# A gated feed-forward kernel on Trainium2: weights of three slots loaded into buffers of their own, sums kept as rows and dealt to GpSimd, two more slots by seven products

## The chip, the cores and the metric

The kernel runs on one core of a Trainium2 chip. A core has five engines that work side by side, each on a queue of its own in order: TensorE (PE, matmuls; PEld is its loading of weights), VectorE (DVE), ScalarE (ACT), GpSimd (POOL) and SyncE (SP, which here issues nearly all DMA transfers). They meet through semaphores. SBUF is the memory that all of them work on, PSUM the eight banks that PE writes its sums to. The metric is the device time of one execution in microseconds (us), median of the runs.

## The reference

The core of it, with x of shape (4, 1024, 512), cond (4, 128), norm_w (512, 128), up_w (4096, 512) and down_w (512, 2048), all f32:

```python
scale = cond @ norm_w.T + 1.0
ms = jnp.mean(x * x, axis=-1, keepdims=True)
h = x * (scale[:, None, :] * jax.lax.rsqrt(ms + EPS))
u = h @ up_w.T
val, gate = jnp.split(u, 2, axis=-1)
h = val * jax.nn.gelu(gate, approximate=False)
hq = act_quant(h)        # 8 bits, one scale per token
wq = weight_quant(down_w)   # -1, 0, 1 times one scale
return hq @ wq.T + x
```

The first product (`h @ up_w.T`) is f32 and is the large part. The second has small integers on both sides.

## The kernel before

**Batches, slots, halves.** The four batches of 1024 tokens are taken one after the other. In each, the 2048 gate and 2048 value features are cut into NJ = 16 slots of 128 gate and 128 value features. A batch's tokens are two halves of TOK = 512. Every f32 operand is kept as a high and a low f16 part and a product is three f16 terms (high by low, low by high, high by high).

**Two ways to compute a slot.** `plain_half` makes one half of a slot directly: twelve matmuls of 512 columns for the gate (`plain`, L1137) into bank A or B, a Gelu on ACT (L1161), twelve for the value into bank E, and a DVE step (L1165) that multiplies both and so empties bank E. A slot is 48 matmuls. `slot` makes both halves at once by seven products of six matmuls (`product`, L1122), 42 a slot, in the manner of Strassen's scheme: it needs sums and differences of the quarters of the weights and of the input, and ACT and DVE copy and add banks between the products (L1200, L1208, L1212; L1220, L1230, L1236, L1239). Of PSUM's banks A and E have two each, B one, and three ("po") serve transposes and small things. In the first batch the slots below SEVEN = 14 are plain and the last two use `slot`; the later batches use `slot` throughout. The plain halves come in the order (0,0), (1,0), (2,0), (0,1), (1,1), (2,1), (3,0), (3,1), (4,0) and so on, (slot, half).

**Weights, once, during the first batch.** For slot j: `w_load` (L747) brings 512 KB of up_w; `w_largest` (L757 on ACT, or L759 on DVE for the first slots) and `w_factor` (L766 to L769) find a power of two for each row; `w_scale` (L788 on ACT, L790 on POOL) multiplies by it; `w_rows` (L813 on ACT, L814 on DVE) splits the result in high and low part and transposes it by DMA into the slot's f16 tile. Slots 0 to 2 are transposed on PE instead (`w_turn`, `w_high`, `w_low`), and `w_evac` (L839) copies the transposed f32 values out of PSUM. `s_sums` (L847 to L850) makes the four sums that the seven products need, from the scaled weights as loaded (slots 3 on) or from what `w_evac` kept (slots 0 to 2); `s_high` (L861, ACT) and `s_low` (L865, DVE or POOL) split them; `s_spill` writes the slot's tile to DRAM, where batches 1 to 3 read it by `s_load_x` and `s_load_y`. The sums of slots 3 to 13 lie in DRAM as rows and are transposed by the DMA that loads them; those of slots 0 to 2, 14 and 15 lie transposed. The natural weights of all slots share three buffers in turn, `W_SLOT`: H[12], H[13] and H[14]. H (18 slots of 128 x 1024 f32) is also the store of the results of the slots.

**Input.** The first batch's x lies in H[4] to H[7]. Its first half is prepared at the start; of the other half `first_sum` takes the sums of squares, `rsqrt` (L982, L983) the root, `first_scale` (L1468 on ACT, L1470 on POOL) scales, `first_turn` (L1475) transposes on PE, `first_high` (L1479, ACT) and `first_low` (L1483, DVE) write the two parts.

**What sets the order.** The program isn't emitted as written. Each call is first recorded by a planner (`Plan`), which knows what depends on what, has a price for each operation (`price`) and a lag for each hand-over between engines (`lag`), works out when each result is needed, and places all steps, PE's foremost. It then tries a list of small alterations, one for each seed in `MENDS`, each of which moves steps ahead of which PE waited in its own replay. The outcome is a fixed order for each engine. Each engine works its list strictly in order: a step that waits holds up everything behind it.

Of the kernel before, what the change touches and what calls it, by code (L numbers as in the profile page):

```python
# [22 lines left out]
P = 128  # L23
# [92 lines left out]
class Plan:  # L116
# [284 lines left out]
    100002, 100010, 100012, 100045, 100056, 100059, 100066, 100072, 100095, 100096, 100105, 100124,  # L401
    100140, 100188, 100274, 100292, 100370, 100398, 100424, 100470, 100489, 100678, 100785, 101115,
    101696, 102543,
# [38 lines left out]
def lag(s, t):  # L442

    if s.eng == t.eng:
        return 0.0
    if s.eng == "PE":
        return 0.2
    return 0.08 if t.eng == "POOL" else 0.05


def price(eng, method, writes, reads, args, kwargs):
# [25 lines left out]
    if method == "reciprocal":  # L477
        return 0.15 + max(0, wide - 8) * 0.0055, False, 0.0
    if wide <= 32:
        return 0.14, not psum, 0.0  # L480
# [40 lines left out]
def glu_quant_kernel(  # L521
# [142 lines left out]
    def cond_scale_rest():  # L664

        n = B - 1
        v = H[:, 9:11].rearrange("p s h t -> p (s h t)")[:, : n * NK * C]
# [42 lines left out]
    def cond_rows():  # L710

        n = NK * B
        pr, v = po_bank("pr", [n, P]), H[:n, 8, 0, 64 : 64 + P]
# [18 lines left out]
    W_SLOT = {1: 12, 2: 13, 0: 14}  # L732
# [3 lines left out]
    def wn(j):  # L736
        return H[:, W_SLOT[j % 3]]

    def wf(j):

        return H[:, 11 if j == 2 else 15 + j % 2].rearrange("p t (n f) -> p (t n) f", n=2)
# [39 lines left out]
    SEVEN = 14  # L781

    def w_scale(j, ts=(1, 0), eng=None):
        eng = eng or (ACT if j >= ROWS else POOL)
# [17 lines left out]
    def a_parts(j):  # L802

        s = s_tile(j)
        return s[:, 5:7], s[:, 3] if j >= ROWS else A21[:, j % 3], s[:, 4]
# [31 lines left out]
    def w_evac(j):  # L837
        for n in range(2):
            ACT.copy(wf(j)[:, 2 * n : 2 * n + 2].rearrange("p n f -> p (n f)"), pw[j][n])  # L839

    def s_sums(j):
        if j >= ROWS:
            v = wn(j).rearrange("p t (n f) -> p t n f", n=2)
            a11, a12, a21, a22 = v[:, 1, 0], v[:, 1, 1], v[:, 0, 0], v[:, 0, 1]
        else:
            a11, a12, a21, a22 = (wf(j)[:, n] for n in range(4))
        DVE.tensor_tensor(sf[:, 0], a21, a22, ALU.add)  # L847
        DVE.tensor_tensor(sf[:, 2], a11, a21, ALU.subtract)
        DVE.tensor_tensor(sf[:, 1], sf[:, 0], a11, ALU.subtract)
        DVE.tensor_tensor(sf[:, 3], a12, sf[:, 1], ALU.subtract)  # L850

    def s_parts(j):
# [3 lines left out]
        s4 = A21[:, j % 3 : j % 3 + 1] if j >= ROWS else s[:, 3:4]  # L856
# [718 lines left out]
    def first_batch(j, sc):  # L1575
# [34 lines left out]
        for f in FIRST_T.get(j, ()):  # L1610
            f()
# [473 lines left out]
```

## Time and profile before

| | us |
|---|---|
| median of 3 runs | 731.36 (731.32 to 731.37) |
| the profiled execution | 731.21 |
| its span | 729.2 |
| busy: PE, DVE, ACT, POOL | 719.0, 616.4, 410.0, 120.5 |

The span is what the profiler's records cover; the execution's own time is 2.0 us longer. The profile's rows are groups of instructions: line, engine, operation, output <- input, shape, count, then busy time in us, the mean of one in ns, and the idle time ahead of them with what ended it. In rows of the timeline the first number is the start, the second the duration, and a bracket gives the wait ahead. The ends of matmuls are modelled, so durations of PE rows overlap the next row; their starts are good. The last batch ends with the second product's tail; the change leaves its code alone.

### The profile page before, as it was taken

What the parts mean: (1) busy time and instruction counts of PE and PEld (TensorE: products, weight loads), DVE (VectorE), ACT (ScalarE), POOL (GpSimd) and SP (SyncE); (2) the same over time, 40 slices, a digit from 0 to 9 for tenths busy, and PEclk for the clock granted to TensorE, in tenths of its full rate; (3) what the DMA queues carried; (4) which work ended last, traced back from release to release, by engine and by line L of the source; (5) the groups of instructions that cost most, each with busy time, mean ns of one, the idle gap of its engine ahead of it and who ended that gap; (6) DMA issues with size and microseconds to landing.
All of it is one profiled execution on the core that took longest, in us unless ns stands there. A gap on an engine that the chain in (4) does not pass through costs nothing.

```text
span 729.2 us, 10150 instructions
## 1 busy us (share of the span) xinstructions
PE 719.0 (99%) x3655; PEld 358.4 (49%) x3655; DVE 616.4 (85%) x916; ACT 410.0 (56%) x671; POOL 120.5 (17%) x116
## 2 busy tenths in 40 slices
PE   8999999999999999999999999999999999999998
PEld 4544444444444446655444445665444444445744
DVE  7988898989898789968789888688879889956898
ACT  5776875773656785554433777733333676332454
POOL 2411222210000004570001300660001000000010
PEclk9999999999999999999999999999999999999999
DMA  7379687999767796777543446669543334443414
GB/s 253 119 236 216 159 227 232 233 251 262 237 208 169 190 184 184 192 161 177 136 129 92 95 101 188 159 156 181 120 101 102 102 101 102 102 101 101 149 44 155
DMA packets 185805, 116.77 MB, mean 160 GB/s; under 512 B 147718, under 2 KB 155287, under 8 KB 185756
## 3 DMA queue, kind: packets, MB, share of 16 engines
q1 hardware_dynamic: 185466, 115.81, 62.3%
q8 instruction: 28, 0.46, 0.3%
q10 hardware_dynamic: 290, 0.33, 0.1%
q14 instruction: 21, 0.17, 0.1%
HBM read 58.15 MB, written 23.09 MB: 111 GB/s over the span
## 4 chain that ended last, share of the span: by engine, by line
PE 83%; DVE 10%; ACT 3%; issue 2%; POOL 1%; DMA 1%; SPq 0%; DVEq 0%; ACTq 0%; POOLq 0%
PE A L1122 33%; PE E L1122 17%; PE po L1394 9%; PE B L1122 8%; PE E L1137 6%; PE B L1137 3%; PE A L1137 3%; DVE H L1315 2%; DVE am L1283 1%; DMA wd<-xr 1%; DVE H L814 1%; ACT H L788 1%; ACT H L813 1%; DVE R L1352 1%; ACT xr L950 1%
## 5 line engine op out<-in xcount | busy, mean ns | idle before, releaser
L1122 PEld LDWEIGHTS <-SXY 128*128 128x128 f16 x2016 | 197.2, 98 | 233.2 <-issue 1.9
L1122 PE MATMUL A<-R,SXY 128*128 128x512 f16 x1140 | 264.0, 379 | 1.0 <-ACT t L1200 0.9
L1122 PE MATMUL E<-R,SXY 128*128 128x512 f16 x570 | 138.7, 379 | 0.0
L1315 DVE TENSOR_TENSOR H<-H,am 128x1024 f32<-128x1024 f32 x64 | 77.6, 1235 | 0.1
L1122 PE MATMUL B<-R,SXY 128*128 128x512 f16 x288 | 70.3, 379 | 0.0
L1256 DVE TENSOR_REDUCE gm<-H 128x512 f32<-128x1024 f32 x56 | 68.9, 1231 | 0.9
L1137 PEld LDWEIGHTS <-SXY 128*128 128x128 f16 x438 | 42.8, 98 | 53.2 <-issue 2.3
L1272 POOL PARTITION_ALL_REDUCE am<-R x8 | 16.6, 2078 | 287.8 <-DVE R L1258 254.9
L1220 DVE SCALAR_TENSOR_TENSOR H<-A,sg,t 128x512 f32<-128x512 f32 x50 | 37.4, 749 | 28.5 <-PE A L1122 27.9
L1200 ACT COPY t<-A 128x512 f32<-128x512 f32 x50 | 29.2, 584 | 56.0 <-PE A L1122 56.0
L1233 ACT ACTIVATE t<-t,sg 128x512 f32<-128x512 f32 x50 | 36.1, 721 | 43.0 <-DVE t L1230 42.5
L1208 ACT COPY B<-A 128x512 f32<-128x512 f32 x50 | 28.5, 571 | 50.7 <-PE A L1122 50.3
L1394 PE MATMUL po<-wd,R 128*128 128x256 fp8e4 (+1 forms) x448 | 56.8, 275 | 0.0
L1217 ACT ACTIVATE t<-B,sg 128x512 f32<-128x512 f32 x50 | 34.3, 687 | 39.0 <-PE B L1122 38.7
L1230 DVE TENSOR_TENSOR t<-E,t 128x512 f32<-128x512 f32 x50 | 34.5, 689 | 24.6 <-PE E L1122 24.1
L1394 PEld LDWEIGHTS <-R 128*128 128x128 bf16 (+1 forms) x480 | 47.0, 98 | 12.8
L1236 DVE TENSOR_TENSOR v<-A,v 128x512 f32<-128x512 f32 x50 | 34.5, 689 | 20.0 <-PE A L1122 17.7
L1137 PE MATMUL E<-R,SXY 128*128 128x512 f16 x210 | 48.9, 379 | 1.1 <-DVE H L1165 1.1
L1212 ACT COPY v<-E 128x512 f32<-128x512 f32 x50 | 29.2, 585 | 29.5 <-PE E L1122 18.4
L1323 ACT ACTIVATE H<-H 128x1024 f32<-128x1024 f32 x38 | 39.8, 1050 | 9.7 <-DVE H L1315 9.6
L1239 DVE SCALAR_TENSOR_TENSOR H<-v,sg,t 128x512 f32<-128x512 f32 x50 | 39.8, 797 | 2.4 <-ACT t L1233 2.1
L1327 ACT ACTIVATE R<-H 128x1024 bf16<-128x1024 f32 x38 | 39.5, 1053 | 0.5
(268 smaller groups left out, 959.8 us busy)
## 6 DMA issues: line engine op xcount, KB each, us to landing
SXY<-s_dram SPq DMA_DIRECT2D x55, 256.0 KB, 2.7
H<-in_L_cond_up_w_dram SPq DMA_DIRECT2D x13, 512.0 KB, 4.0
s_dram<-SXY SPq DMA_DIRECT2D x16, 384.0 KB, 3.1
SXY<-s_dram SPq DMA_DIRECT2D x13, 384.0 KB, 3.2
xr<-in_x_dram SPq DMA_DIRECT2D x19, 256.0 KB, 3.2
out_dram<-xr SPq DMA_DIRECT2D x19, 256.0 KB, 2.2
H<-in_x_dram SPq DMA_DIRECT2D x8, 512.0 KB
SXY<-s_dram SPq DMA_DIRECT2D x29, 128.0 KB, 2.2
```

The lines of the kernel that those rows point to most:

```text
L1122: PE.matmul(o, s[:, w, k, :], xs(l, k), start=start and n == 0, stop=stop and n == len(TERMS) - 1, skip_group_check=True,)
L1137: PE.matmul(ps, a[k // 2][:, w, k % 2, :], XP[:, l, k, h * TOK : (h + 1) * TOK], start=n == 0, stop=n == len(terms) - 1,)
L1220: DVE.scalar_tensor_tensor(h_half(g - 1, 0), prev["A"], gain(g - 1, 0), prev["t1"], ALU.mult, ALU.mult)
L1230: DVE.tensor_tensor(prev["t2"], prev["E"], prev["t2"], ALU.add)
L1233: ACT.activation(prev["t2"], prev["t2"], AF.Gelu, scale=gain(g - 1, 1))
L1236: DVE.tensor_tensor(cur["v"], cur["A"], cur["v"], ALU.add)
L1239: DVE.scalar_tensor_tensor(h_half(g - 1, 1), prev["v"], gain(g - 1, 0), prev["t2"], ALU.mult, ALU.mult)
L1256: DVE.tensor_reduce(gm[0], v, AX.X, ALU.max, apply_absolute_value=True)
L1315: DVE.tensor_tensor(v, v, r.to_broadcast([P, 2, TOK]), ALU.mult)
L1323: ACT.activation(v, v, AF.Copy, bias=MAGIC)
L1327: ACT.activation(q, by_tile(v), AF.Copy, bias=-MAGIC)
L1394: PE.matmul(po, w[:, j], m, start=start and j == 0, stop=stop and j == n - 1, skip_group_check=True,)
```

## The change

There are five edits. The order tables that follow show the two engines whose lists move most.

- `W_SLOT` becomes a list: the natural weights of slots 3, 4 and 5 get H[8], H[9] and H[10], so that their loads need not wait for a buffer of slots 0 to 2. Scratch of the condition (`cond_scale_rest`, `cond_rows`), which lay there, moves into R[:, 1].
- `w_evac` goes, and with it the special case of slots 0 to 2: their sums are made from the scaled weights as loaded and kept as rows in DRAM like those of slots 3 on. So `s_load` transposes for slots 0 to 11 instead of 3 to 13, and the spill of slots 0 to 2 is in three pieces instead of one.
- Work is dealt out anew: `s_sums` runs wholly on POOL for slots 0 to 3 and half on POOL for 4 and 5 (all was on DVE); `w_scale` runs on POOL up to slot 4 (was up to 2).
- SEVEN is 12 instead of 14: slots 12 and 13 of the first batch are made by `slot`, and their sums are transposed ahead of the spill. For slots above 12 `w_rows` stands ahead of `s_all`.
- The planner's numbers in `lag` and `price` and its list of seeds change.

```diff
@@ MENDS @@
-26 seeds from 100002 to 102543
+40 seeds from 23000004 to 23011637
@@ lag @@
+    if s.eng == "PE":
+        return 0.0 if t.eng == "PE" else 0.2
     if s.eng == t.eng:
-        return 0.0
-    if s.eng == "PE":
-        return 0.2
-    return 0.08 if t.eng == "POOL" else 0.05
+        return {"DVE": 0.1, "ACT": 0.08, "POOL": 0.07}.get(s.eng, 0.0) if not s.wait else 0.0
+    return 0.05 if s.wait else 0.13 if t.eng == "POOL" else 0.1
@@ price @@
-        return 0.15 + max(0, wide - 8) * 0.0055, False, 0.0
+        return 0.08 + max(0, wide - 8) * 0.006, False, 0.0
     if wide <= 32:
-        return 0.14, not psum, 0.0
+        return 0.08, not psum, 0.0
@@ cond_scale_rest, cond_rows @@
-        v = H[:, 9:11].rearrange("p s h t -> p (s h t)")[:, : n * NK * C]
+        v = R[:, 1, 4096 : 4096 + n * NK * C]
...
-        pr, v = po_bank("pr", [n, P]), H[:n, 8, 0, 64 : 64 + P]
+        pr, v = po_bank("pr", [n, P]), R[:n, 1, 1536 : 1536 + P]
@@ weights @@
-    W_SLOT = {1: 12, 2: 13, 0: 14}
+
+    W_SLOT = [14, 12, 13, 8, 9, 10, 14, 12, 13] + 3 * [14, 12, 13]
     def wn(j):
-        return H[:, W_SLOT[j % 3]]
-
-    def wf(j):
-
-        return H[:, 11 if j == 2 else 15 + j % 2].rearrange("p t (n f) -> p (t n) f", n=2)
+        return H[:, W_SLOT[j]]
...
-    SEVEN = 14
+    SEVEN = 12
...
-        eng = eng or (ACT if j >= ROWS else POOL)
+        eng = eng or (ACT if j >= 5 else POOL)
...
-        return s[:, 5:7], s[:, 3] if j >= ROWS else A21[:, j % 3], s[:, 4]
+        return s[:, 5:7], s[:, 3], s[:, 4]
...
-    def w_evac(j):
-        for n in range(2):
-            ACT.copy(wf(j)[:, 2 * n : 2 * n + 2].rearrange("p n f -> p (n f)"), pw[j][n])
-
     def s_sums(j):
-        if j >= ROWS:
-            v = wn(j).rearrange("p t (n f) -> p t n f", n=2)
-            a11, a12, a21, a22 = v[:, 1, 0], v[:, 1, 1], v[:, 0, 0], v[:, 0, 1]
-        else:
-            a11, a12, a21, a22 = (wf(j)[:, n] for n in range(4))
-        DVE.tensor_tensor(sf[:, 0], a21, a22, ALU.add)
-        DVE.tensor_tensor(sf[:, 2], a11, a21, ALU.subtract)
-        DVE.tensor_tensor(sf[:, 1], sf[:, 0], a11, ALU.subtract)
-        DVE.tensor_tensor(sf[:, 3], a12, sf[:, 1], ALU.subtract)
+        v = wn(j).rearrange("p t (n f) -> p t n f", n=2)
+        a11, a12, a21, a22 = v[:, 1, 0], v[:, 1, 1], v[:, 0, 0], v[:, 0, 1]
+        (POOL if j < 4 else DVE).tensor_tensor(sf[:, 0], a21, a22, ALU.add)
+        (POOL if j < 4 else DVE).tensor_tensor(sf[:, 2], a11, a21, ALU.subtract)
+        (POOL if j < 6 else DVE).tensor_tensor(sf[:, 1], sf[:, 0], a11, ALU.subtract)
+        (POOL if j < 6 else DVE).tensor_tensor(sf[:, 3], a12, sf[:, 1], ALU.subtract)
...
-        s4 = A21[:, j % 3 : j % 3 + 1] if j >= ROWS else s[:, 3:4]
-        return (s[:, 0:3], sf[:, 0:3]), (s4, sf[:, 3:4])
+        return (s[:, 0:3], sf[:, 0:3]), (A21[:, j % 3 : j % 3 + 1], sf[:, 3:4])
@@ s_spill, s_load_x, s_load_y @@
-        if j < ROWS or j >= SEVEN:
+        if j >= SEVEN:
...
-        s_load(g, 0, Y_FROM, ROWS <= w_of(g) < SEVEN)
+        s_load(g, 0, Y_FROM, w_of(g) < SEVEN)
...
-        if not ROWS <= w_of(g) < SEVEN:
+        if w_of(g) >= SEVEN:
@@ first_batch @@
+        if SEVEN < j and n < NJ:
+            w_rows(n)
         if n < NJ:
             s_all(n)
         if j + 3 < NJ:
             w_scale(j + 3)
-            w_rows(j + 3)
+            if j < SEVEN:
+                w_rows(j + 3)
@@ third_slot, after plain_first @@
-        w_evac(2)
...
-    w_evac(0)
-    w_evac(1)
```

In the tables a row is line, operation, output <- input and shape, with a count where a row repeats; lines of the changed kernel are about nine lower than before. First POOL around the root for the other half of the input (`rs_0_88`). Before:

```order
L790 TENSOR_SCALAR H<-H,iv_96 128x512 x2
L790 TENSOR_SCALAR H<-H,iv_103 128x512
L790 TENSOR_SCALAR H<-H,iv_104 128x512 x2
L983 TENSOR_TENSOR rs_0_88<-ssq_0_87,neghalf 128x4
L1470 TENSOR_SCALAR H<-H,rs_0_88 128x512 x2
L982 TENSOR_SCALAR ssq_114<-ssq_114 128x2
L983 TENSOR_TENSOR rs_115<-ssq_114,neghalf 128x2
```

The same place after the change (L839 to L842 are the sums, L856 the low parts, L1461 `first_scale`):

```order
L789 TENSOR_SCALAR H<-H,iv_103 128x512
L842 TENSOR_TENSOR H<-H 128x256
L856 TENSOR_TENSOR SXY<-H,SXY 128x3x256
L839 TENSOR_TENSOR H<-H 128x256
L840 TENSOR_TENSOR H<-H 128x256
L789 TENSOR_SCALAR H<-H,iv_104 128x512 x2
L974 TENSOR_TENSOR rs_0_88<-ssq_0_87,neghalf 128x4
L856 TENSOR_TENSOR R<-H,R 128x256
L1461 TENSOR_SCALAR H<-H,rs_0_88 128x512
L841 TENSOR_TENSOR H<-H 128x256
L1461 TENSOR_SCALAR H<-H,rs_0_88 128x512
L842 TENSOR_TENSOR H<-H 128x256
```

The two input scalings stood directly behind the root; now a low part and a sum stand between.

Second, ACT from the Gelu of half (1,1) to that of half (2,1). Before:

```order
L1161 ACTIVATE t_0_105<-A_89,sg_78 128x512
L861 CAST R<-H 128x256
L861 CAST R<-H 128x3x256
L813 CAST H<-H 128x4x256
L1161 ACTIVATE t_1_106<-A_91,sg_78 128x512
```

After, from the second step behind the Gelu of (1,1) on (the first is another cast of a high part, `L852 CAST SXY<-H 128x3x256`); L756 is `w_largest`, L787 `w_scale`, L812 `w_rows`, L852 `s_high`:

```order
L852 CAST R<-H 128x256
L756 ACTIVATE R,wam_102<-H 128x512 x2
L756 ACTIVATE R,wam_95<-H 128x512
L812 CAST H<-H 128x4x256 x2
L756 ACTIVATE R,wam_95<-H 128x512
L756 ACTIVATE R,wam_102<-H 128x512
L787 ACTIVATE H<-H,iv_96 128x512
L852 CAST SXY<-H 128x3x256
L787 ACTIVATE H<-H,iv_103 128x512 x2
L787 ACTIVATE H<-H,iv_96 128x512
L756 ACTIVATE R,wam_102<-H 128x512
L1152 ACTIVATE t_1_106<-A_91,sg_78 128x512
```

Three steps stood between the two Gelus; now there are fifteen.

Third, ACT at the entry to slot 12. Before, when slot 12 is plain:

```order
L1161 ACTIVATE t_1_106<-A_89,sg_78 128x512
L788 ACTIVATE H<-H,iv_104 128x512 x2
L813 CAST H<-H 128x3x256
L861 CAST SXY<-H 128x3x256
L1161 ACTIVATE t_0_105<-B_90,sg_78 128x512
L861 CAST R<-H 128x4x256
L757 ACTIVATE R,wam_95<-H 128x512 x2
```

After (L1199 copies bank A to B, L1203 bank E to SBUF, L1191 bank A to SBUF, L1208 is `slot`'s Gelu):

```order
L1152 ACTIVATE t_1_106<-A_89,sg_78 128x512
L852 CAST R<-H 128x4x256
L1199 COPY B_90<-A_91 128x512
L756 ACTIVATE R,wam_95<-H 128x512 x2
L1203 COPY v_120<-E_101 128x512
L1191 COPY t_0_121<-A_91 128x512
L787 ACTIVATE H<-H,iv_96 128x512
L1208 ACTIVATE t_0_105<-B_90,sg_78 128x512
L787 ACTIVATE H<-H,iv_96 128x512
L1199 COPY B_90<-A_89 128x512
```

A cast of 1024 values and the copy to bank B are now neighbours, and three copies out of PSUM stand among the weight steps.

More of the change, by code (lines that the diff above doesn't have):

```diff
@@ L400 @@
 MENDS = (
-    100002, 100010, 100012, 100045, 100056, 100059, 100066, 100072, 100095, 100096, 100105, 100124,
-    100140, 100188, 100274, 100292, 100370, 100398, 100424, 100470, 100489, 100678, 100785, 101115,
-    101696, 102543,
[5 rows of a table added]
 )
```

5 rows, old and new, of the table MENDS are left out of this document.

## The prediction

> **What bounds the kernel now.** I read the page's head first, then busy time by stage, then what TensorE waited for.
>
> ```profile
> span 729.2 us, 10150 instructions
> PE 719.0 (99%) x3655; PEld 358.4 (49%) x3655; DVE 616.4 (85%) x916; ACT 410.0 (56%) x671; POOL 120.5 (17%) x116
> ...
> core 0: us, PE busy (x) PEld busy (x) DVE busy (x) ACT busy (x) POOL busy (x), PEclk, DMA share, GB/s
> 24.00:90.00 66.00, 63.70 (x303) 29.59 (x302) 59.52 (x126) 50.04 (x91) 16.02 (x15) 1.00 0.67 176
> 90.00:146.50 56.50, 56.50 (x263) 25.64 (x262) 51.29 (x89) 38.31 (x69) 14.72 (x10) 1.00 0.93 227
> 146.50:167.20 20.70, 20.70 (x98) 9.41 (x96) 17.57 (x37) 15.75 (x28) 3.40 (x4) 1.00 0.95 251
> ```
>
> TensorE (PE) is busy 99% of the span, so there are two ways to gain: fewer matmuls, or less of the little time in which PE waits. The stage rows say where that time is: 2.3 us of the 66 us from 24 to 90 (first batch, about slots 0 to 6), nothing from 90 to 167.2, where the slots that follow end. There DVE is busy 59.5 of 66 us, ACT 50.0, POOL 16.0: DVE is the next bound, POOL has room. The granted clock is 1.00 in all. What PE waited for, over the whole run (us in total, times, longest):
>
> ```profile
> PE E L1137 <- DVE H L1165: 1.5, 3, 1.1
> PE A L1122 <- ACT t L1200: 0.9, 2, 0.7
> PE B L1137 <- ACT t L1161: 0.6, 1, 0.6
> PE B L701 <- DVE dg L695: 0.4, 1, 0.4
> PE po L685 <- DVE mx L678: 0.2, 1, 0.2
> ```
>
> L1137 is `plain`, L1165 the vector operation that empties bank E of a plain half, L1161 its Gelu. Both of the large waits stand in PE's timeline between 66 and 87 us:
>
> ```profile
> 66.59 2.75 PE L1137 MATMUL A<-R,SXY 128*128 128x512 f16 x12
> 70.43 2.75 PE L1137 MATMUL E<-R,SXY 128*128 128x512 f16 x12 [1.08 <-DVE H L1165]
> ...
> 80.82 2.75 PE L1137 MATMUL E<-R 128*128 128x512 f16 x12
> 84.19 2.75 PE L1137 MATMUL B<-R,SXY 128*128 128x512 f16 x12 [0.62 <-ACT t L1161]
> ```
>
> A group of twelve shows 2.75 us because its last matmul's end is modelled; the cost of a matmul is read from the chain of waits, where nothing is late:
>
> ```profile
> 164.64 2.59 PE E L1137 x12
> 167.23 1.29 PE A L1122 x6
> ```
>
> 2.59/12 = 1.29/6 = 0.216 us a matmul. By starts, 70.43 - 66.59 = 3.84 and 84.19 - 80.82 = 3.37, against 2.59: the two slips are 1.25 and 0.78. Each exceeds its printed wait by 0.16, the modelled end. With L1165's two short waits (0.4) and the two of the condition (0.6) as printed, five gaps, 24 to 90 loses 2.3 + 5 x 0.16 = 3.1 us.
>
> **The change part by part.** Slots 12 and 13 by seven products: 42 matmuls instead of 48 each, so 12 x 0.216 = **-2.6**, sure as long as PE stays the bound there. Beside it each slot adds three ACT copies from PSUM and two DVE additions, and takes none off the path. Prices of these and of what follows, from the groups by form (busy, mean ns, idle ahead):
>
> ```profile
> L847 DVE TENSOR_TENSOR H<-H 128x256 f32<-128x256 f32 x16 | 8.8, 549 | 3.9 <-POOL SXY L865 2.1 <-POOL R L865 1.1 <-issue 0.6
> L848 DVE TENSOR_TENSOR H<-H 128x256 f32<-128x256 f32 x16 | 6.7, 417 | 0.0
> L1165 DVE SCALAR_TENSOR_TENSOR H<-E,sg,t 128x512 f32<-128x512 f32 x27 | 19.8, 741 | 2.3 <-POOL H L1105 2.2
> L1236 DVE TENSOR_TENSOR v<-A,v 128x512 f32<-128x512 f32 x9 | 6.2, 688 | 2.0 <-PE A L1122 2.0
> ...
> L788 ACT ACTIVATE H<-H,iv 128x512 f32<-128x512 f32 x27 | 18.4, 715 | 10.8 <-DVE iv L769 10.6
> L757 ACT ACTIVATE R<-H 128x512 bf16<-128x512 f32 x20 | 12.5, 626 | 0.9 <-DMA H<-in_L_cond_up_w_dram 0.6
> L813 ACT CAST H<-H 128x1024 f16<-128x1024 f32 x11 | 11.5, 1043 | 0.3
> L861 ACT CAST SXY<-H 128x768 f16<-128x768 f32 x10 | 8.3, 827 | 3.4 <-DVE H L849 2.8 <-issue 0.6
> L1208 ACT COPY B<-A 128x512 f32<-128x512 f32 x10 | 5.7, 570 | 5.7 <-PE A L1122 5.3
> L861 ACT CAST R<-H 128x256 f16<-128x256 f32 x12 | 4.9, 404 | 10.5 <-DVE H L850 10.5
> L757 ACT ACTIVATION_READ_ACCUMULATOR R<-H 128x1 f32 x20 | 3.8, 188 | 0.0
> L861 ACT CAST R<-H 128x1024 f16<-128x1024 f32 x2 | 2.1, 1036 | 2.1 <-issue 2.1
> ```
>
> Three copies of 0.57 and two additions of 0.69 fit in the idle time that 146.5 to 167.2 has today (ACT 5.0, DVE 3.1 for two slots: 3.4 and 2.8), only just. At the entry to slot 12 the copy B<-A, for which the next product but one waits, is queued on ACT behind a 1024-wide high part: 1.04 + 0.57 = 1.6 us against the 1.29 of the product that covers it. **+0.3** (0 if the high part runs early, 1.2 if both copies meet such a step).
>
> Sums: twenty of the 24 of slots 0 to 5 go from DVE to POOL. At L848's 0.42 (L847's 0.55 holds waits on POOL) DVE is rid of 20 x 0.42 = 8.4 us; the six evacuations of w_evac (L839, priced like L1208: 3.4) and the four scalings of slots 3 and 4 (2.9) leave ACT. The two engines that the slips of 24 to 90 waited on thus get 8.4 and 6.3 us back where they had 6.5 and 16 idle, against slips of 1.25 at most. I take all five as gone: **-3.1** (ends: 0 and -3.1).
>
> What is late next is what waits for POOL, which gets 20 sums, four scalings and the other half's two input scalings in one row:
>
> ```profile
> L790 POOL TENSOR_SCALAR H<-H,iv 128x512 f32<-128x512 f32 x5 | 3.4, 691 | 8.9 <-DVE iv L769 8.8
> ...
> 26.38 2.94 POOL L1470 TENSOR_SCALAR H<-H,rs 128x512 f32<-128x512 f32 x2
> 302.19 0.72 POOL L1037 TENSOR_TENSOR H<-H 128x256 f32<-128x256 f32 x1
> ...
> 31.09 1.84 ACT L1479 ACTIVATE R<-po,scT 128x512 f16<-128x512 f32 x3 [0.35 <-PE po L1475]
> ...
> 33.91 2.75 PE L1137 MATMUL A<-R,SXY 128*128 128x512 f16 x12
> ```
>
> L1037's 302.19 has the shape of a sum: 0.72 us on POOL. First place: behind POOL's rsqrt, a low part of 256 (about a sum's size, with its lock waits 0.8) and a sum now stand ahead of the second input scaling: 0.8 + 0.7 = 1.5 us later. The high parts L1479 that hang on it end at 31.09 + 1.84 = 32.93 today and are first read at 33.91: 1.0 free. **+0.5** (0 if the two steps run before the rsqrt is ready, 1.0 if ACT's own queue adds to it).
>
> Second place: ACT between the Gelus of halves (1,1) and (2,1), where the order shows one cast of 256 then six w_largest (6 x 0.81), two w_rows (2.1), four scalings (2.9), two casts of 768 and the one of 256 (2.1 together): 12.0 us. With both Gelus (0.68 each) and L1165 (0.74) that is 14.1 from the end of gate (1,1). PE has six groups, 15.5 us, until value (3,1) needs the bank of (2,1); with 0.2 of handing over, 1.2 us are free. The casts wait for POOL's sums of slot 3, and the queue with them: nothing if these are done before, four sums and two scalings (4.3) if all come in a row. The middle is 2.1, and 2.1 - 1.2 = **+0.9** (0 to 3.1).
>
> Other slots, 2 to 11: today's order left slips of 0.1 to 1.2, another order on engines with more idle time leaves some. **+0.3** (0 to 1.2).
>
> Hidden: three early weight loads (512 KB each) in free buffers ahead of slot 3; kept rows, which turn three more slots' loads in batches 1 to 3; six further spill pieces. Their cover:
>
> ```profile
> SXY<-s_dram SPq DMA_TRANSPOSE x58, 3.9
> ```
>
> A turned load lands 3.9 us after issue, within a slot of 42 x 0.216 = 9.07 us; that leaves 5 us before it shows, and if the buffer came free so late, all nine loads would cost their excess. From 90 to 167 the queues are 0.93 to 0.95 busy while PE loses nothing; there the change takes the spills of 12 and 13 from full to two halves. The waits on L1200 (0.9) lie after 263 us, where the order hardly moves. Startup: early loads compete with the input tiles; 0 (-0.3 to +0.5).
>
> Sum on the profiled execution (731.21; span 729.2, the rest lies around it): -2.6 - 3.1 + 0.5 + 0.9 + 0.3 + 0.3 = -3.7, so 727.5. The median of the runs is 0.15 above that execution: **727.6**.
>
> **The rivals.** *All is hidden.* POOL's row is served in time everywhere: 731.4 - 2.6 - 3.1 = 725.7. For it: POOL idle for 50 of 66 us today. Against: its steps are nearly twice DVE's (0.72 to 0.42).
>
> *The gain turns into waits on POOL.* The second place costs its upper end, 3.1, and the first 1.0: 731.4 - 5.7 + 4.1 + 0.6 = 730.4, range 728.8 to 731.5. For it: one ACT queue, twelve steps deep, hangs on POOL. Against: the sums can be made as soon as the weights are scaled, and these come early now.
>
> *DVE and POOL block one another, and it gets slower.*
>
> ```profile
> 90.57 3.00 POOL L1105 TENSOR_TENSOR H<-H 128x1024 f32<-128x1024 f32 x1 [1.67 <-DVE H L1105]
> ...
> 91.39 2.46 DVE L847 TENSOR_TENSOR H<-H 128x256 f32<-128x256 f32 x1
> 94.11 0.41 DVE L849 TENSOR_TENSOR H<-H 128x256 f32<-128x256 f32 x1
> ...
> 318.35 1.18 POOL L1036 TENSOR_TENSOR xt<-xn 128x256 f32<-128x256 f32 x1
> ...
> 318.86 1.21 DVE L1239 SCALAR_TENSOR_TENSOR H<-v,sg,t 128x512 f32<-128x512 f32 x1
> ```
>
> A sum on DVE took 2.46 us while a POOL operation on two SBUF inputs ran (to 93.57), and 0.41 beside none. So the moved sums, 20 x 0.72 = 14.4 us on POOL, hold DVE up for a share f of that time: net -8.4 + 14.4f. At f = 0.58 nothing is gained; at f = 1 the stretch loses 6.0, 731.4 - 2.6 + 6.0 = 734.8, the old slips kept. Slower by over 1.5 us needs f above 0.87. Against: only DVE steps with two SBUF inputs show it, and L1165, the Gelu and PSUM work do not belong to them; at 318, where both engines ran such steps back to back, POOL's 1.18 exceeds 0.72 by 0.46, so they shared the loss. I put f at 0.3.
>
> [...]
>
> **How the numbers follow.** All hidden 0.22 (725.7); the forecast's case 0.50 (726.6 to 728.9, likeliest 727.6); waits on POOL 0.18 (half of it under 729.9); blocking 0.10. Fewer than 2 in 10 lie outside 725.3 to 731.2. 0.2% is 1.5 us, about what can be told from no change, with the bounds at 729.9 and 732.8: faster 0.22 + 0.50 + 0.08 = 0.80, same 0.12 (the rest of the third, 0.02 of the blocking), slower 0.08.
>
> **What would show it.** Right: 12 fewer matmuls; PE's waits on L1165 and L1161 between 24 and 90 gone or under 0.5 together; DVE's busy time there down by some 4 us (8.4 - 14.4 x 0.3), POOL's up by about 15; waits of ACT's casts on POOL sums before about 60. Wrong: PE waits of over 2 us near 57 behind a late cast, sums or low parts on DVE of 1 us and more, PE waits on turned loads after 170, or a start later by more than 0.5.

## The result, and the profile after

The changed kernel takes 723.56 us (median of 4 runs, 723.48 to 723.75), the kernel before 731.37: the ratio is 0.9894 with a 95% interval of 0.9876 to 0.9911, so 7.8 us are gained where 3.8 were forecast, and the time lies below the range that was given. The profiled execution took 723.53 with a span of 721.7. The head of its page, with busy time, share and count of each engine:

```profile
span 721.7 us, 10147 instructions
...
PE 715.4 (99%) x3643; PEld 357.3 (50%) x3643; DVE 609.9 (85%) x899; ACT 407.4 (56%) x665; POOL 135.1 (19%) x139
```

Its stages (start:end, length, then busy time and instructions of PE, PEld, DVE, ACT, POOL, granted clock, DMA share, GB/s):

```profile
0.00:24.00 24.00, 21.10 (x102) 10.80 (x103) 19.36 (x71) 12.63 (x27) 11.74 (x19) 1.00 0.81 273
24.00:90.00 66.00, 66.00 (x319) 31.19 (x317) 62.89 (x112) 48.84 (x89) 33.19 (x34) 1.00 0.86 221
90.00:146.50 56.50, 56.50 (x264) 25.59 (x263) 47.67 (x91) 40.39 (x73) 10.48 (x8) 1.00 0.92 215
256.00:392.00 136.00, 136.00 (x740) 72.31 (x739) 118.46 (x156) 71.72 (x125) 41.92 (x43) 1.00 0.64 154
```

And all that TensorE waited for over the whole run:

```profile
PE A L1482 <- DVE H L579: 1.3, 1, 1.3
PE B L1171 <- ACT R L1470: 0.8, 1, 0.8
PE po L1466 <- DVE H L1461: 0.6, 1, 0.6
PE B L703 <- DVE dg L697: 0.2, 1, 0.2
```

All four waits that are left lie in the first 24 us, and TensorE is busy for 66.00 of the 66 us from 24 to 90 and for 136.00 of 136 later. The gain therefore divides so: 12 matmuls at 0.216, 2.6 us; the five slips of the first batch, 3.1; the slips at 263.4, 397.6 and 399.7, 0.37 + 0.31 + 0.83 = 1.5. That is the 7.2 by which VectorE's last step comes sooner (725.67 before, 718.46 after). The rest, 0.6, lies behind that step (0.2 inside the span, 0.25 outside it) and in the difference between the profiled execution and the median (0.1). The start is no part of it: the gate of half (0,1) began at 33.91 before and at 33.92 after.

VectorE (DVE), which gave up 20 sums, is not less busy between 24 and 90 but more: 62.9 us against 59.5. GpSimd (POOL) doubled, from 16.0 to 33.2.

### The profile page after: what moved, and what is told of

Read it like the earlier page. It is cut to its first block, busy times and chain, and to the rows that moved or that the text cites. A ratio compares the mean times of both kernels' runs of the same rounds, so it can differ in the third digit from the quotient of the medians.

```text
span 721.7 us, 10147 instructions
## 1 busy us (share of the span) xinstructions
PE 715.4 (99%) x3643; PEld 357.3 (50%) x3643; DVE 609.9 (85%) x899; ACT 407.4 (56%) x665; POOL 135.1 (19%) x139
## 4 chain that ended last, share of the span: by engine, by line
PE 96%; DVE 3%; ACT 1%; issue 0%; POOL 0%; DVEq 0%; POOLq 0%
PE A L1113 37%; PE E L1113 19%; PE B L1113 9%; PE po L1385 9%; PE E L1128 8%; PE A L1128 5%; PE B L1128 4%; DVE H L1306 1%; PE A L1334 1%; PE E L1334 1%; PE A L1482 1%; PE B L1385 0%; DVE am L1274 0%; PE po L1466 0%; PE A L1171 0%
## 5 line engine op out<-in xcount | busy, mean ns | idle before, releaser
L1113 PE MATMUL A<-R,SXY 128*128 128x512 f16 x1164 | 269.8, 379 | 0.0
L1113 PE MATMUL E<-R,SXY 128*128 128x512 f16 x582 | 141.6, 379 | 0.0
L1113 PE MATMUL B<-R,SXY 128*128 128x512 f16 x300 | 72.9, 379 | 0.0
L1263 POOL PARTITION_ALL_REDUCE am<-R x8 | 15.3, 1908 | 284.7 <-DVE R L1249 250.3
L1211 DVE SCALAR_TENSOR_TENSOR H<-A,sg,t 128x512 f32<-128x512 f32 x52 | 39.0, 750 | 29.3 <-PE A L1113 28.9
L1199 ACT COPY B<-A 128x512 f32<-128x512 f32 x52 | 29.6, 570 | 53.1 <-PE A L1113 52.7
L1191 ACT COPY t<-A 128x512 f32<-128x512 f32 x52 | 30.4, 585 | 50.4 <-PE A L1113 48.1
L1208 ACT ACTIVATE t<-B,sg 128x512 f32<-128x512 f32 x52 | 35.8, 688 | 40.8 <-PE B L1113 40.6
L1203 ACT COPY v<-E 128x512 f32<-128x512 f32 x52 | 30.4, 586 | 31.1 <-PE E L1113 16.5
L1230 DVE SCALAR_TENSOR_TENSOR H<-v,sg,t 128x512 f32<-128x512 f32 x52 | 41.8, 804 | 2.9 <-ACT t L1224 2.7
L1128 PE MATMUL E<-R,SXY 128*128 128x512 f16 x180 | 41.3, 379 | 0.0
```

Of the source, the lines that this page charges most:

```text
L1113: PE.matmul(o, s[:, w, k, :], xs(l, k), start=start and n == 0, stop=stop and n == len(TERMS) - 1, skip_group_check=True,)
L1128: PE.matmul(ps, a[k // 2][:, w, k % 2, :], XP[:, l, k, h * TOK : (h + 1) * TOK], start=n == 0, stop=n == len(terms) - 1,)
L1208: ACT.activation(cur["t1"], pb, AF.Gelu, scale=gain(g, 1))
L1211: DVE.scalar_tensor_tensor(h_half(g - 1, 0), prev["A"], gain(g - 1, 0), prev["t1"], ALU.mult, ALU.mult)
L1230: DVE.scalar_tensor_tensor(h_half(g - 1, 1), prev["v"], gain(g - 1, 0), prev["t2"], ALU.mult, ALU.mult)
```

## The experiments

Each run came with runs of the kernel before on the same chip, whose medians were 731.1 to 731.6. Starts differ a little from chip to chip (of the first 24 us TensorE was busy for 21.10 in the changed kernel's first profile and for 20.63 in that of its second run), so differences are taken from the ratios to before (times 731.4, against the 0.9894 of the changed kernel) where nothing else is said. The interval of such a ratio is 1 us or more to each side: smaller differences rest on the traces, on where TensorE slips. The changed kernel was also run again beside the last group:

> The changed kernel again, as the base for runs on this chip: 723.5 to 724.2 (the start may differ by 0.5 from chip to chip).

It took 723.72 us, ratio 0.9886 (0.9871 to 0.9901).

Two ways of making a variant were used. In some the planner's order is kept word for word and a few steps are given to another engine or moved after planning, so that nothing else stands elsewhere. Where the steps themselves change, a new order had to be found: seeds were tried one after the other and those kept that made the planner's own replay shorter. Such an order may be worse than the one that came with the change.

### One part undone, the order kept

The 20 sums back on VectorE, and the four scalings back on ScalarE (ACT), each at the places where the plan has them (abridged):

```diff
-    book.emit(book.order())
+    steps = book.order()
+    for s in steps:                       # sums_dve
+        if s.eng == "POOL" and s.line in s_sums:
+            s.do = nc.vector.tensor_tensor
+    book.emit(steps)
...
+    for s in last_four_POOL_scalings:     # scale_act
+        w, _, r = s.args[:3]
+        s.do, s.args, s.kwargs = nc.scalar.activation, (w, w, AF.Copy), {"scale": r}
```

> The changed kernel with the 20 sums that it gives to GpSimd run by VectorE instead, each at the place in VectorE's row that the plan gave it; nothing else is moved. Theory 1 (the first batch is free of waits because VectorE was relieved): VectorE is busy 62.9 of the 66 us from 24 to 90 after the change, so some 3 idle; about 15 of the sums lie there, 6 us at 0.41, while the 6.4 us that it loses to GpSimd's lock there falls away. Net it is near zero on the average, but the sums stand at places where another engine ought to work beside it: 724.5 to 727, PE waits on L1156 back. Theory 2 (the order did it, and the engine of the sums is immaterial): 723.3 to 723.9. Theory 3 (the lock costs more than the sums): below 723.3.

> The changed kernel with the four weight scalings of slots 3 and 4 on ScalarE instead of GpSimd, at their places, nothing else moved: 4 x 0.62 from start to start = 2.5 us more on ACT between about 38 and 50, where ACT is idle for 2.4, 0.6 and 2.0 us. Theory 1 (relief of the engines by the new division of work made the waits go; half (2,1) ends 0.6 us before its bank is needed): 724 to 725.5. Theory 2 (order and slack decide, the division is immaterial): 723.4 to 723.8.

Sums on VectorE: 727.24 us, ratio 0.9946 (0.9931 to 0.9961), 3.8 us over the changed kernel. Scalings on ScalarE: 724.51, 0.9904 (0.9889 to 0.9919), 0.7 over. In the first, 2.4 of it is there by 52 us, before the first plain slots are through (the condition's small matmul L703 came at 52.04 instead of 49.66). A slip of 0.8 at 38.9 is a part of this, and some can be the chip's start: the changed kernel, run again on another chip, had L703 at 50.09. A second slip of 0.8 follows at 60.9. In the run with the scalings on ScalarE it is one slip of 0.8 at 58.9, the bank of half (2,1). All three slips are waits on L1156, so theory 1 of each holds as far as the order stays, with 727.24 lying 0.2 above its range. One supposition there failed: without the sums on GpSimd VectorE's steps between 24 and 90 are still lengthened by 4.6 us, where they were by 6.4 (more on this below).

The 20 sums on GpSimd in the kernel before, the other way round:

> The kernel before with the same 20 sums on GpSimd instead of VectorE at the places where they stand, nothing else moved: this part of the change alone. Theory 1 (relief of VectorE is what counts): the waits on L1165 at 44, 48 and 70 us go, 2.0 of the 3.1, and 729 to 730 comes out. Theory 2 (what counts is the order that was made for it): the sums take 0.72 instead of 0.41 in a chain of four, ACT's casts behind them come later, 731.4 to 734.

It is slower: 735.04, ratio 1.0048 (1.0034 to 1.0062), above the range of theory 2 too. TensorE's timeline there, and two of ScalarE's casts ahead of it:

```profile
67.31 2.75 PE L1137 MATMUL A<-R,SXY 128*128 128x512 f16 x12
73.48 4.44 PE L1137 MATMUL E<-R,SXY 128*128 128x512 f16 x12 [3.42 <-DVE H L1165]
...
55.58 0.83 ACT L861 CAST SXY<-H 128x768 f16<-128x768 f32 x1 [3.54 <-POOL H L848]
...
59.88 0.41 ACT L861 CAST R<-H 128x256 f16<-128x256 f32 x1 [2.57 <-POOL H L850]
```

ScalarE's casts wait for the sums, which now take 0.72 and more each in a chain (3.54, 2.57 and, at 65.02, 2.05 us), the Gelu behind them and with it L1165 come later, TensorE waits for 3.42 us, and the twelve matmuls behind take 4.44 instead of 2.75. From start to start that is 4.28 us (73.48 to 77.76) instead of 2.59, 1.7 more. So the same dealing of sums gains 3.8 us in one order and loses 3.5 in another.

### The order alone, and the division with no seeds

```diff
 # no_seeds: changed kernel
-MENDS = (23000004, ... 40 seeds)
+MENDS = ()
 # order_alone, order_alone2: kernel before, with the changed lag() and price()
-MENDS = (100002, ... 26 seeds)
+MENDS = (31000003, ... 34 seeds)          # order_alone
+    book.emit([book.steps[n] for n in ORDER])   # order_alone2: found from before's own order
```

> The changed kernel with an empty list of seeds: the planner's first placement. Theory A (the order is what removed the waits): several waits of 0.5 to 3 us, 727 to 735; a wait of over 2 us is followed by matmuls at half rate, some 1.7 us more. Theory B (the program has slack enough and the seeds add little): 723.6 to 725.5.

> The program of before (its own division of work, buffers and 14 plain slots) with the changed lag and price numbers and with a list of 34 seeds found for it in the way that the lists were made: alterations kept where the planner's own replay becomes shorter. So only the order differs from before. Theory A (the order took the waits away, the first batch's and those at 263 and 397 to 400): of the 3.1 and 1.5 us most goes, 726.7 to 728.5. Theory B (relief of VectorE and ScalarE did it in the first batch, the order only at 263 to 400): 729 to 730.5, waits on L1165 stay between 24 and 90.

> The program of before with the changed lag and price numbers and an order found from before's own, so that its start stays. If the order alone could take away all waits behind 24 us: 731.4 - 3.1 - 1.5 = 726.8. By the earlier such run, whose waits behind 24 us came to 1.8 instead of 5.0: 731.4 - 3.2 = 728.2, 727.3 to 729. If the division of work is needed for that: 729.5 to 731.

The changed program in the planner's first placement takes 733.4 us, ratio 1.0023 (1.0008 to 1.0038): slower than before. Its waits are back, at the same kinds of places. What TensorE waited for most, and the timeline at two of these:

```profile
PE A L1108 <- ACT t L1186: 3.3, 2, 2.0
PE E L1123 <- DVE H L1151: 2.2, 2, 1.5
```

```profile
75.94 2.75 PE L1123 MATMUL E<-R 128*128 128x512 f16 x12 [1.50 <-DVE H L1151]
...
397.21 4.44 PE L1108 MATMUL A<-R,SXY 128*128 128x512 f16 x12 [2.03 <-ACT t L1186]
```

The old program in a new order takes 729.83 (0.9971, interval 0.9954 to 0.9989) with a start 2 us late and a slip of 1.0 at 84.7, behind a Gelu and not behind the vector step that theory B named, and 729.28 (0.9963, 0.9948 to 0.9977) in the second try. The second try lies between the cases of its expectation. In that run every slip behind 59 us is gone but for 0.1, those at 263 to 400 too; in the first batch one large wait is left, with a slip of 0.3 at 25.6, where there were five:

```profile
50.78 2.75 PE L1137 MATMUL E<-R 128*128 128x512 f16 x12 [2.05 <-DVE H L1165]
```

So a new order alone gets some 2 us on the old program, the late 1.5 among them, and the changed program without a sought order gets less than nothing. What the new division is worth where both orders are sought in the same way is read from this group: with 14 plain slots the changed program takes 0.9932 of before (below), the old one 0.9971, some 2.9 us more, of which about 2 are its late start. The old program with no seeds was not run. That it could not be ordered without a wait in the first batch is not shown, only that it was not found here.

### The late waits: one chain

The slip at 263.4 was not followed further. The larger of the two at 397.6 and 399.7, in TensorE's timeline of the kernel before:

```profile
399.71 1.46 PE L1122 MATMUL A<-R,SXY 128*128 128x512 f16 x6 [0.67 <-ACT t L1200]
```

They were first put down to TensorE's own order, which is odd at that place in the kernel before: products of slot 37 stand ahead of product 6 of slot 36. They were put in regular order, nothing else moved:

```diff
+        rank = {(6, 36): 0, (0, 37): 1, (4, 37): 2, (1, 37): 3}   # (product, slot)
+        # the steps of these four products change places in this order
```

> The kernel before with TensorE's order alone made regular at one place in the third batch: product 6 of slot 36 ahead of products 0, 4 and 1 of slot 37 instead of behind product 0, and these three one after the other. That is how the changed kernel has it. Theory (the waits at 397.6 and 399.7, 0.31 and 0.83, come from this odd order alone, because the two groups on bank A follow each other so that the copy out of it cannot hide): 731.4 - 1.1 = 730.2. Rival (the copies are late there because ACT and VectorE are, and the wait moves on): 731.2 to 731.5.

That was wrong. It takes 733.9, ratio 1.0032 (1.0019 to 1.0045). The wait grew, because the odd order had worked around it. TensorE and ScalarE of that run:

```profile
399.24 4.29 PE L1122 MATMUL A<-R,SXY 128*128 128x512 f16 x12 [2.28 <-ACT t L1200]
...
398.60 0.59 ACT L1200 COPY t<-A 128x512 f32<-128x512 f32 x1 [4.74 <-DVE H L1239]
```

The copy had waited for L1239, and L1239 for more. In the kernel before VectorE and GpSimd have, from the second token half's last maximum on:

```profile
389.16 0.69 DVE L1258 TENSOR_TENSOR R<-R,gm 128x512 f32<-128x512 f32 x1
...
389.95 1.78 POOL L1272 PARTITION_ALL_REDUCE am<-R  x1 [11.17 <-DVE R L1258]
...
391.76 0.43 DVE L1277 TENSOR_SCALAR am<-am 128x512 f32<-128x512 f32 x1 [0.71 <-POOL am L1272]
392.23 3.39 DVE L1283 RECIPROCAL am<-am 128x128 f32<-128x128 f32 x4
395.65 1.22 DVE L1315 TENSOR_TENSOR H<-H,am 128x1024 f32<-128x1024 f32 x1
...
397.45 0.68 DVE L1319 TENSOR_SCALAR R<-H 128x1024 bf16<-128x1024 f32 x1
398.24 0.75 DVE L1239 SCALAR_TENSOR_TENSOR H<-v,sg,t 128x512 f32<-128x512 f32 x1
```

L1239 writes a place in H that still holds the previous batch's result, until L1315 and L1319 have scaled and rounded it, and these need the reciprocals of the maximum. The two all-reduces stand at 376.97 and 389.95, 13 us apart; in the changed kernel they stand 4.5 apart, since the last maximum comes about a slot sooner:

```profile
368.90 1.81 POOL L1263 PARTITION_ALL_REDUCE am<-R  x1 [34.11 <-DVE R L1249]
373.40 1.78 POOL L1263 PARTITION_ALL_REDUCE am<-R  x1 [2.69 <-DVE R L1249]
```

So the two steps of that maximum were moved up in the kernel before, with TensorE's regular order:

```diff
+        # VectorE: the last L1256 and L1258 ahead of the second all-reduce go
+        # directly behind the L1220 that follows the first half's last L1258
```

> The kernel before with TensorE's regular order at slots 36 and 37 (as in the earlier run that came out slower) and with two steps of VectorE moved: the last pair's maximum of the second token half (L1256, L1258) stands 11 us earlier, ahead of the first half's scaling, where VectorE waits for GpSimd anyway. Theory: the chain that ended in the waits at 397.6 and 399.7 begins there: maximum, GpSimd's all-reduce L1272, four reciprocals, L1315 and L1319, which free the place in H that L1239 writes, which frees the buffer that ACT's copy L1200 fills, for which TensorE waits. Started earlier by the two steps' 1.9 and the 0.7 that VectorE waited for the all-reduce, the chain is 2.6 us ahead, and the 2.28 us wait of the regular order is gone, with it the half-rate matmuls: 1.1 below before, so 730.0 where before is 731.1. Rival (the chain is held by something else): 731 to 734.

The mechanism is right, its size is not. The wait fell from 2.28 to 0.89 us and the matmuls behind it run at full rate, 1.7 us by the ratios below the run with the regular order alone:

```profile
398.43 2.75 PE L1122 MATMUL A<-R,SXY 128*128 128x512 f16 x12 [0.89 <-ACT t L1200]
```

But the chain came only 1.4 us earlier, not 2.6, because the new place left VectorE waiting at other steps, and the time is 731.84, ratio 1.0009 (1.0000 to 1.0018), no better than before with its workaround. The new orders, which move the whole chain, gain these slips; this single exchange did not. Whether every step of the chain has to move for that was not tried.

### The slots by seven products

```diff
-    SEVEN = 12
+    SEVEN = 14        # plain_14
+    SEVEN = 10        # seven_10; seven_10b with another order
```

> The changed kernel with SEVEN = 14, slots 12 and 13 plain again, and 27 seeds found for it likewise. By the term for the matmuls: 723.6 + 12 x 0.216 = 726.2, with up to 0.7 more where the order found is worse. Rival (the copies and additions of two seven-product slots took back part of the gain, or the freed banks gained more): 723.5 to 725.3, or above 727.

> The changed kernel with SEVEN = 10: slots 10 and 11 of the first batch by seven products too, and 48 seeds found for it. If the term for matmuls goes on: 723.6 - 2.6 = 721.0. From 90 to 146.5 the changed kernel leaves VectorE 8.8 and ScalarE 16.1 us idle, and two such slots add 2.8 and 3.4. Rival (the two engines, or the parts of the input that seven products need, are late so early in the batch): waits on copies out of A or E after 120 us, 722.5 to 726.

> SEVEN = 10 again, with another order: as in the changed kernel for what that starts in its first 60 us, and found likewise for the rest. The earlier run of SEVEN = 10 lost some 4 us before 54 us, mostly in the first 14, and nearly nothing behind that. If the term for the matmuls holds and the start is the changed kernel's: 723.6 - 2.6 = 721.0 (720.5 to 722). Rival (slots 10 and 11 by seven products make VectorE and ScalarE late): 722.5 to 725.

With 14 plain slots 727.1 us, 0.9932 (0.9911 to 0.9953): 2.8 over the changed kernel by the ratios, where 2.6 had been reckoned; 0.4 of it is a slip behind 24 us. With 10 and an order of poor start, 725.16 (0.9906); behind 73 us that run had no slip at all. With the changed kernel's start, 721.84 us (721.62 to 721.92), ratio 0.9871 (0.9857 to 0.9884). It beats both kernels: 1.9 us below the 723.72 of the changed one by the medians, whose runs lie clear of each other (721.62 to 721.92, 723.39 to 724.01); by the ratios it is 1.1 to 1.7, with intervals that overlap. The 2.6 of the matmuls are there, less two slips of 0.3 and 0.6 near 61 us that this order has, the longer of them behind this wait:

```profile
PE E L1128 <- DVE H L1156: 0.4, 1, 0.4
```

### Evacuation, buffers, and the sums in an order of their own

```diff
 # with_evac, evac_and_buffers: w_evac, wf() and the three-way s_sums of before again
+    def w_evac(j):
+        for n in range(2):
+            ACT.copy(wf(j)[:, 2 * n : 2 * n + 2].rearrange("p n f -> p (n f)"), pw[j][n])
 # old_buffers, evac_and_buffers
-    W_SLOT = [14, 12, 13, 8, 9, 10, 14, 12, 13] + 3 * [14, 12, 13]
+    W_SLOT = 6 * [14, 12, 13]
 # sums_dve_own
-        (POOL if j < 4 else DVE).tensor_tensor(sf[:, 0], a21, a22, ALU.add)
+        DVE.tensor_tensor(sf[:, 0], a21, a22, ALU.add)     # and the other three
```

> The changed kernel with w_evac and the sums of slots 0 to 2 from the transposed values again, kept transposed in DRAM in one piece; all else as changed, with an order found for it likewise, starting from the changed kernel's. Six copies of 0.5 us from start to start come back on ACT, 3.0 us between about 24 and 45. Theory 1 (that relief of ACT counts, slack at half (2,1) is 0.6): 724 to 726. Theory 2 (ACT has idle time enough there, and turned loads in the later batches cost nothing either way): 723.3 to 724.

> The changed kernel with the natural weights of slots 3 to 5 in the three shared buffers again (in turn, as before); all else as changed, with an order found for it likewise, starting from the changed kernel's. Theory 1 (own buffers are what lets POOL and DVE begin on slots 3 to 5 while slots 0 to 2 are still in use): the loads of slots 3 to 5 wait for the sums of slots 0 to 2, which are on POOL now; waits of TensorE between 24 and 70 of 1.5 to 6 us in all, 725 to 730. Theory 2 (loads were hidden before, the first use lay 20 us behind them): 723.4 to 724.6.

> The changed kernel with two parts undone that belong together: natural weights of slots 3 to 5 in the three shared buffers, and the sums of slots 0 to 2 from values that w_evac copies out of PSUM, so that the buffers are free early. SEVEN = 12 and the sums on GpSimd stay; the order was found likewise, from the changed kernel's. Theory 1 (own buffers let the weight work of slots 3 to 5 start early; shared ones bind it to slots 0 to 2): waits of TensorE of 1.5 to 5 us between 24 and 90, 725 to 729. Theory 2 (buffers immaterial given an order): 723.6 to 724.6, as with w_evac alone, which came out 0.7 above the changed kernel.

> The changed kernel with all sums on VectorE and an order found for that program, from the changed kernel's. In the order made for GpSimd this cost 3.7 us, 2.4 of it before 52 us. Theory 1 (dealing the sums to GpSimd is what freed the first batch): 725 to 727. Theory 2 (an order fitted to the division is what counts; what VectorE gains by 20 sums it loses nearly again to GpSimd's lock): 723.3 to 724.5.

With w_evac again: 724.25, 0.9904 (0.9890 to 0.9917), 0.5 over the 723.72 of the changed kernel and 0.7 to 1.3 by the ratios, with one slip of 0.2 behind 24 us (at 34.6); the rest, if it is more than the chip's start, lies before that. The time is at the lower end of theory 1's range, but there is no wait near half (2,1), which it rests on: six copies on ScalarE cost about a microsecond at most, not three.

The shared buffers could not be told apart. In old_buffers (729.26) the sums of slots 0 to 2, which come late in the program, read weights of slots 3 to 5 that have taken their place; the kernel computes something else there and its waits are not those of the question. It does show that the two edits belong together: without w_evac the natural weights must stay until the sums are made. Both undone, evac_and_buffers, came out at 732.79 (1.0012, interval 1.0002 to 1.0023), but all of the loss lies before 60 us, in an order whose start is bad and outside the range of either theory (TensorE busy 15.3 of the first 24 us; the granted clock was 0.89 there and 0.96 from 24 to 90). This is inconclusive: no order of a good start was found for it, though the kernel before has one with the same buffers.

Sums all on VectorE in an order made for that: 724.8 us, 0.9902 (0.9887 to 0.9918), 1.1 above the changed kernel, where the same change in the other order cost 3.8. All of the 1.1 is there by 51 us (L703 at 51.24 against 50.09). The stage from 24 to 90 in this run:

```profile
24.00:90.00 66.00, 66.00 (x321) 31.48 (x320) 63.31 (x131) 47.90 (x86) 20.73 (x19) 1.00 0.80 216
```

and in the changed kernel run beside it:

```profile
24.00:90.00 66.00, 66.00 (x321) 31.45 (x319) 62.76 (x114) 48.41 (x88) 33.01 (x34) 1.00 0.87 218
```

VectorE does 131 instructions in the one and 114 in the other, and is nearly as busy, 63.3 and 62.8 us. Most of what it is spared in sums comes back as longer steps: those beside GpSimd's are lengthened by 6.4 us in the changed kernel and by 1.5 here. Both orders leave TensorE no wait in this stage, and the time lies between the two theories.

## Why the prediction was right or wrong

**Right.** The matmul term: 2.6, with the change of SEVEN measured at 2.8 one way (2.4 without its slip) and, with its two slips added back, 2.7 the other. That all five slips of 24 to 90 go (3.1; of the two waits of the condition that the prediction counts among them with 0.6, one of 0.44 lies at 6.86, and the other is 0.15, but its total of 2.3 is that of the stage). That the start, the turned loads and the early weight loads cost nothing: no wait on a load behind 24 us.

**Wrong, the term for new waits (2.0).** This is half of the miss, and the case called "all is hidden" (725.7) is what happened there. The largest, 0.9 at the bank of half (2,1), was summed from mean durations. ScalarE there, with VectorE's and TensorE's steps that follow:

```profile
42.06 0.69 ACT L1152 ACTIVATE t<-A,sg 128x512 f32<-128x512 f32 x1
42.65 0.82 ACT L852 CAST SXY<-H 128x768 f16<-128x768 f32 x1
44.10 0.41 ACT L852 CAST R<-H 128x256 f16<-128x256 f32 x1 [0.63 <-POOL H L842]
46.51 0.63 ACT L756 ACTIVATE R<-H 128x512 bf16<-128x512 f32 x1 [2.00 <-DVE sw L765]
...
53.24 1.95 ACT L787 ACTIVATE H<-H,iv 128x512 f32<-128x512 f32 x3
...
55.70 0.67 ACT L1152 ACTIVATE t<-A,sg 128x512 f32<-128x512 f32 x1
...
56.40 0.75 DVE L1156 SCALAR_TENSOR_TENSOR H<-E,sg,t 128x512 f32<-128x512 f32 x1 [0.21 <-ACT t L1152]
...
57.76 2.75 PE L1128 MATMUL E<-R,SXY 128*128 128x512 f16 x12
```

From 42.65 to 55.70 are 13.05 us, of which ScalarE waited 2.63; the steps took 10.4, not 12.0. The printed duration of one holds about 0.1 us that overlaps the next: three scalings of 0.715 take 1.95. So the queue bore waits of 2.6 (2.1 had been supposed, but on sums; 2.0 of them were for VectorE's power-of-two factors) and was through at 57.15. TensorE's six groups also took 16.0 us instead of 15.5, with two small matmuls of the condition between them. The bank was free 0.6 ahead of need.

The 0.5 at the input's other half took the right delay and the wrong margin. In the changed kernel GpSimd's row there, with ScalarE's high parts, the last of which the prediction did not show:

```profile
26.31 0.70 POOL L1461 TENSOR_SCALAR H<-H,rs 128x512 f32<-128x512 f32 x1
...
27.68 2.21 POOL L1461 TENSOR_SCALAR H<-H,rs 128x512 f32<-128x512 f32 x1
...
31.10 1.84 ACT L1470 ACTIVATE R<-po,scT 128x512 f16<-128x512 f32 x3
32.82 0.70 ACT L1470 ACTIVATE R<-A,scT 128x512 f16<-128x512 f32 x1
```

The two steps between delay the scalings by 1.4, where 1.5 had been reckoned, but the root came 0.6 sooner, and GpSimd was through at 29.89 instead of 29.32. TensorE turns the tile that waits for it last, from 30.79, so 0.9 were still free, and the high parts start where they did (31.10, before 31.09). Behind these less is free than the prediction read: its row holds three of four parts, and the fourth ends at 33.5 before and after, 0.4 ahead of the 33.9, not 1.0.

The 0.3 each for slots 2 to 11 and for slots 12 and 13 did not occur; the 1024-wide high part ran at 141.42, before slot 12's first product began at 143.22, not in front of the copy at 144.72.

**Wrong, "the waits on L1200 lie after 263 us, where the order hardly moves".** This is the step that put the time outside the range: 1.5 us. The prediction put the gain behind 263 us at nothing; the three slips there (0.37, 0.31, 0.83) went. The change rewrote the planner's numbers and seeds for the whole program, and a maximum came about a slot sooner. The range reached only to what the first batch could give. The 2.0 of the new waits, this 1.5 and the 0.6 around the end of the profile make up the miss of some 4 us.

**Wrong, the reason for the right 3.1.** VectorE's busy time was to fall by 4 us; it rose by 3.4. Twenty sums fewer are 8.1 us as printed, but some 6 us of other work of the batch were drawn into the stage (two more maxima among them), and twelve steps that stand beside GpSimd's are lengthened, by 6.4 us in all beside the shortest of their kind (before: no step by over 0.1). So VectorE got no room, and the slips went all the same; with the sums on VectorE and an order of its own none came back either. Undone one by one, each with an order sought for it, neither the sums nor w_evac nor the two slots by seven products brought slips of over 0.2 back in this stage; the old program kept some in both orders found for it (1.0 and 2.5 in all). Which parts of the new division an order without waits needs stays open.

The share f of GpSimd's time that costs VectorE was put at 0.3, for the moved sums. Of the 6.4 us only 1.6 fall beside sums, 0.14 of their 11.1 us in this stage. Low parts account for 3.1, L1096 (L1105 before) for 1.35 and a weight scaling for 0.4. Low parts ran on GpSimd in this stage before as well, and lengthened no step of VectorE's there; and with the sums taken off GpSimd in the same order (sums_dve) 4.6 us stay. The rival of blocking was right that VectorE is held up and wrong in what holds it: mostly not the moved sums, but where the order puts VectorE's steps beside GpSimd's. It lost because VectorE did not decide the stage.

## What to carry to other kernels

Where every engine's order is fixed in advance, a change of the dealing and a change of the order could not be priced apart here: the same 20 sums gained 3.8 us in one order and lost 3.5 in another, and one change of the planner's numbers touches waits 300 us away from the code that was edited. Queue sums belong to start-to-start distances, not to mean durations (three scalings of 0.715 us on the mean took 1.95 here). Before a wait is put down to the engine that it names, follow the chain back until a step is reached that could have started earlier: here it began at a maximum 10 us and seven steps ahead, and TensorE's odd order was not its cause but its remedy.

## What the runs showed of the hardware

A wait of TensorE of two microseconds and more cost more than itself in three places. Behind waits of 2.03 us (no_seeds, to 397.21), 2.28 (before_regular, to 399.24) and 3.42 (before_sums_pool, to 73.48) the next twelve matmuls took 4.28, 4.13 and 4.28 us from start to start instead of 2.59, so 1.5 to 1.7 us more. In before_regular seven of them had started by 402.0, 2.76 us after the first began, where thirteen would have at one in 0.216: about half the rate. The mean granted clock of the three profiled executions was 0.998, 0.998 and 0.997, against 1.000 in the kernels before and after. Behind waits of 1.50 (no_seeds, to 75.94), 1.08 (before, to 70.43) and 0.89 (before_max_early, to 398.43) the twelve took 2.58 or 2.59, and behind 2.05 (order_alone2, to 50.78) they took 2.59 too: the 2 us in the expectation of no_seeds is no bound that these runs show. Nor was a wait of 2 us needed: in evac_and_buffers the granted clock was 0.89 in the first 24 us and 0.96 from 24 to 90, and TensorE's longest waits in that whole run were two of 1.8 us and one of 1.5. What decided between these cases is not shown.

In the changed kernel more of VectorE's steps lasted longer beside GpSimd than the operations on two SBUF inputs to which the prediction confined it. Steps on 128 x 2 values, 0.22 and 0.15 us alone (L774 and L631), took 1.61, 0.72 and 0.84 beside it, ending within 0.04 of GpSimd's step each time; L631 reads one tile alone:

```profile
37.43 0.84 DVE L631 TENSOR_SCALAR wam<-wam 128x2 int32<-128x2 int32 x1
...
53.55 1.61 DVE L774 TENSOR_SCALAR sg<-sw,dx 128x2 f32<-128x2 f32 x1
...
58.77 0.72 DVE L774 TENSOR_SCALAR sg<-sw,dx 128x2 f32<-128x2 f32 x1
...
36.59 1.64 POOL L856 TENSOR_TENSOR R<-H,R 128x768 f16<-128x768 f32 x1
...
53.41 1.74 POOL L856 TENSOR_TENSOR SXY<-H,SXY 128x768 f16<-128x768 f32 x1 [3.58 <-ACT SXY L852]
...
58.74 0.73 POOL L842 TENSOR_TENSOR H<-H 128x256 f32<-128x256 f32 x1
```

So one of these small steps, L774, which makes the factor that the Gelu takes, lasted 1.61 us instead of 0.22 beside a GpSimd step of 1.74, and another, L631 in the chain to the factors that weights are scaled with, 0.84 instead of 0.15 beside one of 1.64. Where the recorded texts speak of a lock, they put two numbers to it: the 6.4 us are the lengthenings of VectorE's steps beside GpSimd's between 24 and 90, and the 0.8 of a low part of 256 is the mean of six in the kernel before (0.83, the shortest 0.67). What holds a step up is not shown.
